# A two-layer PixArt block on one core: cross-attention's transfers in quarters, biases added one stage later, packed modulations

## The chip, the cores and the metric

The kernel runs on one core of one Trainium2 chip. The metric is the device time of one execution in microseconds. The core has five engines with an instruction queue each: TensorE (PE) for matrix products, VectorE (DVE), ScalarE (ACT), GpSimd (POOL) and SyncE (SP), which here only issues transfers (DMA). An engine works through its own queue in order and waits for semaphores where an instruction needs the work of another engine or of a transfer. POOL and ACT issue transfers too.

## The reference, cut to what matters

All numbers are float32. B = 8 batches, N = 512 rows, H = 512, 16 heads of 32, a context of 77 rows per batch, MLP width 2048.

```python
# layer 0 (stage x): adaptive layer norm, cross-attention to the context, residual
ss = silu(cond) @ W_ss + b_ss; scale, bias = split(ss, 2)     # for q and for kv
xq  = (1 + scale_q) * ln(x)  + bias_q
xkv = (1 + scale_kv) * ln(ctx) + bias_kv
x = x + (attention(xq @ Wq + bq, xkv @ Wkv + bkv) @ Wp + bp)
# layer 1
shift_a, scale_a, gate_a, shift_m, scale_m, gate_m = split(silu(cond) @ W_mod + b_mod, 6)
# stage a: self-attention
x = x + gate_a * (self_attention(ln(x) * (1 + scale_a) + shift_a) @ W_proj + b_proj)
# stage c: cross-attention
x = x + (attention(ln(x) @ W_qc + b_qc, ln(ctx) @ W_kvc + b_kvc) @ W_cproj + b_cproj)
# stage m: MLP
h = gelu((ln(x) * (1 + scale_m) + shift_m) @ W_mlp1 + b_mlp1)
x = x + gate_m * (h @ W_mlp2 + b_mlp2)
```

## The kernel before

**Stages.** Setup (0 to about 78 us of the span) computes the modulations of layer 0 and the keys and values of the context for layer 0. Then come stage x (to about 420), stage a (to about 1320), stage c (to about 1680) and stage m. Each stage runs over the 8 batches. The residual x lives in DRAM between stages, one buffer `xa` per batch (512x512). A stage loads a batch's x into an SBUF tile (`x_x`, `x_a`, `x_c`, `x_m`), and adds its result to `xa` with accumulating transfers that POOL issues (L734, L1094).

**Who sets the order.** Most engines' orders are written out by hand: the code's order is the engine's order (`manual_schedule`). In setup only PE's is, and in the context part too; in stages x and c all but SP's. What is not written out is set by the planner.

**Modulations.** `mod_half` (L95) and `Modulation.block` (L1400) compute silu(cond) @ W for 512 columns: four products with a stationary matrix of 128x8 (`csT`), one behind the other into the same 8 rows of PSUM, a copy on ACT, then four transposes and an addition of the bias on DVE. The two blocks of gates go to DRAM (`gate_a`, `gate_m`) instead. There are ten blocks: four in setup, four in stage x, two in stage c.

**Setup.** The context's rows (`cx`) come over ACT's queue, the weights over SP's. DVE takes the statistics of `cx` (L376), and copies `csT` out of PSUM (L169). `context_x` normalises, transposes and modulates the context, and multiplies it by the value weights (`cv_ps_x`, L359) and the key weights (`ckT_ps_x`, L408).

**Stages x and c** (`cross_phase`, L593). The loop is over 32 groups: batch b, group fc of four heads. A group computes scores, maxima, exponentials, sums (`total`, DVE), the division (POOL), a turn (DVE), and the outputs of the group before. Beside it run products with seven multiplications instead of eight (`Seven`), for the queries of the next batch or the projection of an older one, or a block of modulations (`fill`). The x of batch b+3 is loaded by one transfer at group 1, the value rows of the next batch (`load_values`) at group 2, stage x copies the input to `xa` at group 1, and `add_bias` (L743) adds the output bias to `xa` with one accumulating transfer of 1024 KB at group 3.

**Stage a** (`self_phase`, L1013). Again 32 groups. In a group, PE makes the scores of the next group for four tiles of 128 keys (`scores`, L1120), in two PSUM tiles that are free again when ACT has copied them (L1138) and DVE has taken the running maxima (`mx_a`, L1140). The maxima travel to DRAM (`mxd`), POOL issues eight accumulating transfers that subtract them from the scores in SBUF (`shift`, L1174), ACT takes exponentials (L1183), POOL and DVE add up (L1190). In group 2 the next batch's x is turned, and after that `load_x` (L1033) brings the x of the batch after it into the one tile `x_cur`; in group 3 DVE takes its statistics (L205), between the maxima of key tile 1 and those of key tile 2. The projection's result is biased on DVE (L1088), gated on POOL (L1091) and added to `xa` (L1094).

**Stage m.** `hidden` and `outputs` use products in quadrants with seven multiplications (`Quad`): a Quad takes up to four PSUM banks out of six in turn, and DVE empties them. `outputs` makes eight results of 128x256 (`result`, L1688): DVE reads PSUM into `res` (three buffers), adds the bias; POOL multiplies by the gate (L1696) and adds to the piece `xr` of the residual (L1697); SP stores `xr` (L1698), and after each of the first four results loads the piece for four results later (L1685) into one of the four `xr` buffers. The next batch's x is loaded at the start of `outputs` (L1538), normalised after the second set of products, turned on DVE and with 16 small transfers (L1551).

Of the kernel before, what the change touches and what calls it, by code (L numbers as in the profile page):

```python
# [11 lines left out]
F32 = mybir.dt.float32  # L12
# [12 lines left out]
SCALE = HD ** -0.5  # L25
RSQRT_SEED = float(0x5F3759DF)
# [3 lines left out]
def tile_pixart_block(ctx: ExitStack, tc: tile.TileContext, a: dict, out: bass.AP):  # L30
# [50 lines left out]
    csT = const.tile([P, KC, B], F32, name="csT")  # L81
# [13 lines left out]

    def mod_half(u, w, bname, dst, pool, psp, tag):
# [3 lines left out]
        for k in range(KC):  # L100
            nc.tensor.matmul(
                ps[:B, :], lhsT=csT[:, k, :], rhs=w[:, k, :], start=(k == 0), stop=(k == KC - 1)
            )
        m = pool.tile([B, H], F32, tag="mod", bufs=2, name=f"mod_{bname}_{u}")
        mark = nc.scalar.copy(m, ps[:B, :])
        yield
        pt = psp.tile([P, H], F32, tag=tag, name=f"modT_ps_{bname}_{u}")
        for j in range(KC):
            nc.tensor.transpose(pt[:, ts(j, B)], m[:, ts(j, P)], ident[:B, :B])
# [11 lines left out]
    def load_context(pool):  # L121
        cx = pool.tile([P, CT, H], F32, tag="cx", bufs=1, name="cx")
        rows = ctx_in.rearrange("b s h -> (b s) h")
        nc.scalar.dma_start(
            out=cx[:, : CT - 1, :],
            in_=rows[: (CT - 1) * P, :].rearrange("(t p) h -> p t h", p=P),
        )
        nc.scalar.dma_start(out=cx[:RL, CT - 1, :], in_=rows[(CT - 1) * P :, :])
        return cx
# [19 lines left out]

    kv_x = tc.alloc_tile_pool(name="kv_x", bufs=1)  # L150
    sp = tc.alloc_tile_pool(name="setup", bufs=1)
    with tc.tile_pool(name="setup_ps", bufs=2, space=PSUM) as spp:
# [11 lines left out]
        nc.scalar.activation(cs, c_sb, AF.Silu)  # L164

# [3 lines left out]
        nc.vector.tensor_copy(csT.rearrange("p k b -> p (k b)"), cp[:, : KC * B])  # L169

        w_ss_kv = [load_w("L0_xcond_Wss_kv", u) for u in range(2)]
        halves = [
            mod_half(u, w_ss_kv[u], "L0_xcond_bss_kv", mod_kv, sp, spp, "ps") for u in range(2)
        ]
        next(halves[0])
        bp = spp.tile([P, H], F32, tag="ps", name="bcol_ps")
        nc.tensor.transpose(bp[:, :n_cols], brow, ident[:n_cols, :n_cols])
        nc.vector.tensor_copy(bcol, bp[:, :n_cols])

# [7 lines left out]
        w_ss_q = [load_w("L0_xcond_Wss_q", 0)]  # L187
        w_l0 = [None, load_w("L0_xcond_Wkv", 1)]
        w_l0[0] = load_w("L0_xcond_Wkv", 0)
        w_ss_q.append(load_w("L0_xcond_Wss_q", 1))  # L190
# [158 lines left out]
    with tc.tile_pool(name="ps_s", bufs=2, space=PSUM, reuse_waits="tile") as ps_s:  # L349
# [17 lines left out]
        def context_x(eps, w_k, w_v, bkv, work, prep, cx):  # L367
# [4 lines left out]
            mv = small.tile([P, CT, 2], F32, tag="cmv", bufs=1, name="cmv_x")  # L372
            nc.gpsimd.memset(mv, 1.0)
            for t, n in enumerate(parts):
                bn = small.tile([P, 6], F32, tag="st", name=f"cst_x_{t}")
                nc.vector.bn_stats(bn[:n], cx[:n, t, :])  # L376
                nc.vector.bn_aggr(mv[:n, t, :], bn[:n])
# [3 lines left out]
            for k in range(KC):  # L381
# [14 lines left out]
                if k % 2:  # L396
                    mark = run(mod_half(k // 2, w_ss_q[k // 2], "L0_xcond_bss_q", mod_q, prep, ps_m, "m"))
            vd = dram.tile([R, H], F32, name="cvd_x")
            for t in range(CT):
# [3 lines left out]
                ))  # L403
            for j in range(KC):
# [12 lines left out]
            return kT, vd, last, mark, mv  # L417
# [168 lines left out]
        def cross_phase(  # L586
# [8 lines left out]
            bq, bkv, bo = names  # L595
            work = stack.enter_context(tc.tile_pool(name=f"work_{nm}", bufs=2, reuse_waits="tile"))
# [12 lines left out]
            def load_values(b):  # L609

                vr = st[b]["vr"] = work.tile([P, KB, H], F32, tag="vr", bufs=2, name=f"vr_{nm}{b}")
                whole = KB if b + 1 < B else KB - 1
                for i in range(QB):
                    at = vd[b * S : b * S + whole * SQ, :]
                    nc.sync.dma_start(
                        out=vr[ts(i, SQ), :whole, :], in_=at.rearrange("(k s) h -> s k h", s=SQ)
                    )
                    if whole < KB:
                        nc.sync.dma_start(
                            out=vr[i * SQ : i * SQ + S - whole * SQ, whole, :],  # L620
                            in_=vd[b * S + whole * SQ : (b + 1) * S, :],
                        )
# [89 lines left out]
            def project(b, j, room=None):  # L712
# [28 lines left out]
                )  # L741

            def add_bias(b):  # L743
                nc.gpsimd.dma_start(
                    out=x_dst[nm][b], in_=bo.partition_broadcast(N), accum_op=ALU.add
                )
# [120 lines left out]
            g.most(lambda: run(head[0]))  # L867
# [12 lines left out]
            ahead = behind_o = nothing  # L880
            for n in range(B * KC):
# [4 lines left out]
                if fc == 1 and more:  # L886
                    side = ahead
                elif b > 0 and fc == (2 if more else 1):
# [27 lines left out]
                now.scores()  # L916
                if pending:
                    pending.c22()
                    pending.mm(3)
                    pending.take("c12")  # L920
# [24 lines left out]
                now.total(0)  # L945
# [33 lines left out]
                if fc == 0 and more:  # L979
                    ahead = x_sums(b + 1, nc.gpsimd)  # L980
                    pump(ahead)
                if fc == 1 and b + 3 <= B:
                    load = next_x(nc.sync)
                if fc == 2 and more:
                    load_values(b + 1)
                if fc == 1 and modulated:
                    with tc.issue_after(load.ins):
                        nc.sync.dma_start(out=x_dst[nm][b], in_=x_src[nm][b])
                if fc == 3:
                    add_bias(b)  # L990
# [22 lines left out]
        def self_phase(w, bo_row, work, work_2, ctx_c):  # L1013
# [8 lines left out]
            x_cur = x_sb["a", 0]  # L1022
            sums = [xpool.tile([P, 4, N], F32, tag="x", name=f"sum_a{i}") for i in range(2)]
# [9 lines left out]
            def load_x(b):  # L1033
                nc.scalar.dma_start(
                    out=x_cur, in_=x_src["a"][b].rearrange("(t p) d -> p t d", p=P)
                )

# [43 lines left out]
            def project(b, t):  # L1081
                if t == 0 and b + 1 < B:
# [704 lines left out]
```

## Time and profile before

| | us |
|---|---|
| median of 3 runs (2483.24 to 2492.29) | 2483.47 |
| the profiled execution | 2482.09 |
| its span, first to last instruction | 2480.3 |
| PE busy, in all | 2355.1 |
| PE busy, setup, 0 to 78 | 57.4 |
| PE busy, stage x, 78 to 420 (342 us) | 326.3 |
| PE busy, a stretch of stage a, 560 to 1160 (600 us) | 581.3 |
| PE busy, stage c, 1320 to 1680 (360 us) | 333.1 |
| PE busy, stage m, 1800 to 2400 (600 us) | 600.0 |

The span is that of one profiled execution. A busy time is the sum of an engine's instructions; the clock column of the windows is the share of TensorE's full clock that the chip granted (1.00 is full). Timelines give the start and length of merged instructions, the tile written and the tiles read, and in brackets how long the engine had been idle and who released it. Transfers of the queue q0 (software, issued by POOL) move 176 MB, those of q1 (SP) 108 MB.

### The profile page before, as it was taken

The numbers are of one execution on the slowest core, as the hardware profiler recorded it, in microseconds if no ns is written. First come the engines' busy times: TensorE is split into PE (matmuls) and PEld (weight loads), VectorE is DVE, ScalarE is ACT, GpSimd is POOL, SyncE is SP. The second block draws the span as 40 slices with busy tenths as digits, with TensorE's granted clock in tenths as the row PEclk, the third lists the DMA queues.
The fourth block names the chain that finished last, engine by engine and source line by source line (L and its number), as shares of the span: only waits on it lengthen the run. The fifth ranks groups of instructions, "written<-read, shape, count | busy, mean of one in ns | idle before, by whom it ended". The sixth has DMA issues, their size and how long they took to land. (4 is left out here: it accounts for less than half of the span.)

```text
span 2480.3 us, 44498 instructions
## 1 busy us (share of the span) xinstructions
PE 2355.1 (95%) x17701; PEld 1502.9 (61%) x17701; DVE 1690.7 (68%) x2922; ACT 1168.3 (47%) x2043; POOL 1179.3 (48%) x1210
## 2 busy tenths in 40 slices
PE   7899999889999999999988899998999999999998
PEld 3567776323333333333234677777888888888887
DVE  3577785588888888888745777766656556655563
ACT  1366663577777777776652565652121121121120
POOL 2357674366776777867664566654202102012011
PEclk9999999999999999999999899999999999999999
DMA  7456647498999999999996465554211111112010
GB/s 262 145 118 145 146 67 123 98 183 169 194 190 182 199 172 193 190 180 181 199 218 168 88 112 83 78 85 115 58 32 56 45 45 56 34 47 66 23 51 26
DMA packets 142595, 298.99 MB, mean 121 GB/s; under 512 B 15668, under 2 KB 46468, under 8 KB 142260
## 3 DMA queue, kind: packets, MB, share of 16 engines
q0 software_dynamic: 59424, 176.23, 41.5%
q1 hardware_dynamic: 77023, 108.16, 14.6%
q10 hardware_dynamic: 5941, 11.76, 1.4%
q8 instruction: 139, 2.28, 0.4%
q14 instruction: 68, 0.56, 0.1%
HBM read 252.39 MB, written 61.54 MB: 127 GB/s over the span
## 5 line engine op out<-in xcount | busy, mean ns | idle before, releaser
L1696 POOL TENSOR_TENSOR res_m<-res_m,gate_m 128x256 f32<-128x256 f32 x64 | 49.9, 780 | 638.8 <-DVE res_m L1694 638.8
L1174 POOL DMA_DIRECT2D e_a<-mxd_a x256 | 249.7, 2043 | 155.1 <-DMA mxd_a<-mxT_a 142.8
L1183 ACT ACTIVATE e_a<-e_a 128x1024 f32<-128x1024 f32 x256 | 265.8, 1058 | 87.1 <-DMA e_a<-mxd_a 86.2
L1138 ACT COPY e_a<-sT_a 128x1024 f32<-128x1024 f32 x256 | 254.9, 1010 | 94.0 <-DVE mx_a L1140 45.6
L1630 ACT ACTIVATE hT<-hT,bcol 128x512 f32<-128x512 f32 x128 | 91.9, 721 | 239.1 <-DVE hT L1605 231.0
L1190 POOL TENSOR_TENSOR sum_a<-e_a,e_a 128x1024 f32<-128x1024 f32 x64 | 153.7, 2445 | 103.5 <-ACT e_a L1183 103.1
L1190 POOL TENSOR_TENSOR sum_a<-sum_a,e_a 128x1024 f32<-128x1024 f32 x64 | 171.7, 2693 | 3.8 <-ACT e_a L1183 3.8
L1140 DVE TENSOR_TENSOR mx_a<-sT_a,mx_a 128x1024 f32<-128x1024 f32 x128 | 151.0, 1218 | 31.7 <-PE sT_a L1120 28.7
L1120 PE MATMUL sT_a<-qT_a,kT_a 32*128 32x512 f32 x1024 | 150.1, 640 | 12.3 <-ACT e_a L1138 10.6
L1200 PE MATMUL o_ps_a<-e_a,v 128*32 128x512 f32 x1024 | 148.5, 611 | 9.2 <-ACT e_a L1183 9.0
L807 POOL TENSOR_TENSOR p_x<-p_x,sm_x 128x616 f32<-128x616 f32 x64 | 83.6, 1421 | 103.3 <-DVE sm_x L803 81.7
L1597 PE MATMUL q_ps_h<-x_m,w_L_xcond_W_mlp 128*128 128x256 f32 x512 | 132.3, 381 | 0.0
L1597 PE MATMUL q_ps_h<-xT_m,w_L_xcond_W_mlp 128*128 128x256 f32 x512 | 131.7, 380 | 0.0
L304 PE MATMUL q_ps_a<-xnT_a,w_L_xcond_W_qkv 128*128 128x512 f32 x256 | 124.1, 613 | 6.9 <-ACT xnT_a L1043 6.9
L807 POOL TENSOR_TENSOR p_c<-p_c,sm_c 128x616 f32<-128x616 f32 x64 | 83.0, 1403 | 99.0 <-ACT xnT_c L293 40.9
L1218 DVE RECIPROCAL rz_a<-z_ps_a 128x512 f32<-128x512 f32 x32 | 107.4, 3358 | 31.3 <-PE z_ps_a L1211 31.3
L1597 PE MATMUL q_ps_h<-x_m,w_s 128*128 128x256 f32 x512 | 122.0, 381 | 5.3 <-DVE w_s L1522 4.5
L304 PE MATMUL k_ps_a<-xnT_a,w_L_xcond_W_qkv 128*128 128x512 f32 x256 | 120.5, 608 | 0.0
L312 PE MATMUL v_ps<-w_L_xcond_W_qkv,xnT_a 128*128 128x512 f32 x256 | 120.0, 612 | 0.0
L312 PE MATMUL proj_ps_a<-w_L_xcond_W_proj,oT_a 128*128 128x512 f32 x256 | 117.9, 604 | 1.4 <-DVE oT_a L1221 1.4
L1597 PE MATMUL q_ps_y<-w_L_xcond_W_mlp,h_s 128*128 128x256 f32 x512 | 113.1, 379 | 0.0
L1597 PE MATMUL q_ps_y<-w_L_xcond_W_mlp,hT 128*128 128x256 f32 x512 | 113.1, 379 | 0.0
(421 smaller groups left out, 5271.8 us busy)
## 6 DMA issues: line engine op xcount, KB each, us to landing
e_a<-mxd_a POOLq DMA_DIRECT2D x256, 512.0 KB, 11.6
xa<-in_L_xcond_bp_dram POOLq DMA_DIRECT2D x8, 1024.0 KB, 14.6
xa<-res_x POOLq DMA_DIRECT2D x32, 256.0 KB, 5.1
xa<-res_a POOLq DMA_DIRECT2D x32, 256.0 KB, 14.3
x_c<-xa SPq DMA_DIRECT2D x8, 1024.0 KB
w_L_xcond_W_mlp<-in_L_xcond_W_mlp_dram SPq DMA_DIRECT2D x8, 1024.0 KB
xa<-in_L_xcond_b_cproj_dram POOLq DMA_DIRECT2D x8, 1024.0 KB, 15.2
xa<-res_c POOLq DMA_DIRECT2D x32, 256.0 KB, 5.2
```

The source lines that it names most:

```text
L304: nc.tensor.matmul(ps, lhsT=w[:, k, ts(j, P)], rhs=xT[k], start=(k == 0), stop=(k == KC - 1))
L312: nc.tensor.matmul(ps, lhsT=xT[k][:, cols], rhs=w[:, k, :], start=(k == 0), stop=(k == KC - 1))
L807: nc.gpsimd.tensor_tensor(v, v, self.sm[i].unsqueeze(3).to_broadcast([P, 2, NT, S]), ALU.mult)
L1120: nc.tensor.matmul(sc[h // 2][:, h % 2, :], lhsT=kT[ts(h, HD), ts(k, P)], rhs=qT[ts(h, HD), :], start=True, stop=True,)
L1138: nc.scalar.copy(self.e[k][i], sc[i])
L1140: nc.vector.tensor_tensor(self.mx[1 - i], sc[1 - i], self.e[0][1 - i] if k == 1 else self.mx[1 - i], ALU.max,)
L1174: nc.gpsimd.dma_start(out=self.e[k][i].rearrange("p h n -> p (h n)"), in_=self.mxd[2 * i : 2 * i + 2, :] .rearrange("h n -> (h n)").partit ...
L1183: nc.scalar.activation(self.e[k][i], self.e[k][i], AF.Exp)
L1190: engine.tensor_tensor(sum_i, self.e[0][i] if k == 1 else sum_i, self.e[k][i], ALU.add)
L1200: nc.tensor.matmul(self.po[ts(h, HD), :], lhsT=vt[:, self.fc * P + h * HD : self.fc * P + (h + 1) * HD], rhs=self.e[k][h // 2][:, h % 2, : ...
L1218: nc.vector.reciprocal(r, self.pz)
L1597: nc.tensor.matmul(self.banks[n][:, half], lhsT=lhsT, rhs=rhs, start=(k == 0), stop=(k == len(pairs) - 1),)
```

## The change

- **Transfers of stages x and c.** The load of x, of the value rows and the copy to `xa` are cut in four, one part for each group of a batch, each held by a dependency (`paced`) until a certain sum of that group is done on DVE. SP's order in these stages is now written out too.
- **Biases.** `add_bias` of `cross_phase` is gone: `xa` no longer has the output bias of stages x and c. Stage a adds `bp` to its x on POOL, and to its result through a row `gate * b_proj + bp` per batch (`shift`). Stage m adds `b_cproj` with accumulating transfers: four into each `x_cur`, one into each piece `xr`. The first x of the next stage, loaded ahead in group loop 5, gets its bias by one transfer a group (`owed`).
- **Modulations.** `csT` is padded to 32 columns; the four products of a block write four groups of 32 rows of PSUM, each on its own. A matrix of ones and zeros (`pick`, 128x8) adds the four groups up in the products that also turn the columns (`mod_columns`). The second block of stage c moves from group (1, 0) to (1, 1).
- **Setup.** PE's and DVE's order is written out: `csT` is copied before the context's statistics; the context comes first on SP's queue; both modulations of kv start before the bias columns; the modulations of q stand between the value products.
- In the first batch of stages x and c the sums of the next batch's xT go to DVE instead of POOL.

```diff
+    def mod_parts(ps, w):
         for k in range(KC):
             nc.tensor.matmul(
-                ps[:B, :], lhsT=csT[:, k, :], rhs=w[:, k, :], start=(k == 0), stop=(k == KC - 1)
+                ps[ts(k, CG), :], lhsT=csT[:, k, :], rhs=w[:, k, :], start=True, stop=True
             )
+    def mod_columns(ps, m):
+        for j in range(KC):
+            nc.tensor.matmul(ps[:, ts(j, B)], lhsT=m[:, ts(j, P)], rhs=pick, start=True, stop=True)
...
-        nc.scalar.dma_start(
+        nc.sync.dma_start(
             out=cx[:, : CT - 1, :],
...
+    def paced(after, dma):
+        if after is not None:
+            tc.add_manual_dep(
+                dma.ins, after.ins.name,
...
+    def add_row(dst, row):
+        nc.gpsimd.dma_start(out=dst, in_=row.partition_broadcast(P), accum_op=ALU.add)
...
+        nc.vector.memset(csT, 0.0)
+        nc.vector.tensor_reduce(
+            pick, ident.rearrange("p (g c) -> p c g", c=CG)[:, :B, :], AX.X, ALU.add
+        )
...
+        context_rows(cx, c_mv)
         next(halves[0])
+        next(halves[1])
...
             for t in range(CT):
                 run(values_c(
...
+                for half in queries_mod[t - 1 : t]:
+                    next(half)
+                for half in queries_mod[t - 2 : t - 1] if t > 1 else []:
+                    run(half)
...
-                    ahead = x_sums(b + 1, nc.gpsimd)
-                    pump(ahead)
-                if fc == 1 and b + 3 <= B:
-                    load = next_x(nc.sync)
-                if fc == 2 and more:
-                    load_values(b + 1)
-                if fc == 1 and modulated:
-                    with tc.issue_after(load.ins):
-                        nc.sync.dma_start(out=x_dst[nm][b], in_=x_src[nm][b])
-                if fc == 3:
-                    add_bias(b)
+                    ahead = x_sums(b + 1, nc.gpsimd if b else nc.vector)
+                    pump(ahead, 1 if b else 0)
+                if b + 3 <= B:
+                    if fc == 0:
+                        ahead_x[b] = next_x_tile()
+                    dst, src = ahead_x[b]
+                    paced(half, nc.sync.dma_start(out=dst[:, fc, :], in_=src[ts(fc, P), :]))
+                    if b + 3 == B:
+                        owed = dst[:, fc, :], bo
+                if fc and more:
+                    load_values(b + 1, [fc - 1], last)
+                elif b and fc == 0:
+                    load_values(b, [QB - 1], last)
+                if modulated:
+                    for t in [fc] if more else [[0, 1], [2, 3], [], []][fc]:
+                        paced(last, nc.sync.dma_start(out=x_dst[nm][b][ts(t, P), :], in_=x_src[nm][b][ts(t, P), :]))
...
+            def add_bias(t):
+                nc.gpsimd.tensor_tensor(x_cur[:, t, :], x_cur[:, t, :], bp_row, ALU.add)
+
+            def gate_and_shift(b):
+                g = st[b]["g"] = gate_rows(gate_a, b, work, "a")
+                shift = st[b]["shift"] = work.tile([P, H], F32, tag="shift", name=f"shift_a{b}")
+                nc.gpsimd.tensor_tensor(shift, g, bo_row, ALU.mult)
+                nc.gpsimd.tensor_tensor(shift, shift, bp_row, ALU.add)
...
-                        nc.vector.tensor_tensor(tmp, pr, bo_row, ALU.add)
+                        nc.vector.tensor_tensor(tmp, pr, st[b]["g"], ALU.mult)
                         def add():
-                            nc.gpsimd.tensor_tensor(tmp, tmp, st[b]["g"], ALU.mult)
+                            nc.gpsimd.tensor_tensor(tmp, tmp, st[b]["shift"], ALU.add)
...
                 for k in range(1, NT):
                     g.shift(k)
                 flush(0)
                 flush(1)
+                if fc == 3 and b + 2 < B:
+                    for t in range(NT):
+                        add_bias(t)
+                if fc == 0 and b:
+                    gate_and_shift(b - 1)
...
-                    (0, 1): lambda: mod.block(4), (1, 0): lambda: mod.block(5),
+                    (0, 1): lambda: mod.block(4), (1, 1): lambda: mod.block(5),
...
                     in_=x_src["m"][b][ts(i, P), :].rearrange("(t c) d -> c t d", c=SQ),
                 )
+            for t in range(NT):
+                add_row(x_cur[:, t, :], bc)
...
                 nc.sync.dma_start(out=xr, in_=x_src["m"][b][ts(t + 2 * r, P), ts(c, H2)])
+                add_row(xr, bc[ts(c, H2)])
                 pieces[t, r, c] = xr
```

## The prediction

> **What bounds the kernel now.** I read the page's totals first, then the windows by stage, then the timelines of single engines inside one round of each stage.
>
> ```profile
> PE 2355.1 (95%) x17701; PEld 1502.9 (61%) x17701; DVE 1690.7 (68%) x2922; ACT 1168.3 (47%) x2043; POOL 1179.3 (48%) x1210
> 0.00:78.00 78.00, 57.40 (x193) 28.46 (x194) 21.64 (x68) 13.61 (x22) 19.18 (x31) 1.00 0.65 225
> 160.00:420.00 260.00, 255.35 (x4228) 199.59 (x4228) 197.12 (x370) 155.35 (x430) 169.40 (x219) 1.00 0.62 113
> 660.00:760.00 100.00, 97.31 (x428) 32.09 (x430) 84.81 (x99) 73.19 (x82) 75.64 (x56) 1.00 0.97 186
> 1800.00:2000.00 200.00, 200.00 (x929) 176.05 (x928) 117.11 (x278) 38.19 (x63) 24.86 (x32) 1.00 0.18 49
> ```
>
> TensorE (PE) is idle for only 125 us of 2480.3: 20.6 of them in the first 78 us, 15.7 in cross-attention x, 27 in cross-attention c (1320 to 1680), about 3 per batch in self-attention, none in the MLP until its tail. So little can be won, and whatever makes PE wait in self-attention or the MLP is paid in full.
>
> Self-attention, third batch, fourth group (VectorE DVE, then GpSimd POOL, then PE):
>
> ```profile
> 750.48 0.68 DVE L205 BATCH_NORM_STATS2 st_a<-x_a 128x6 f32<-128x512 f32 x1
> 753.58 0.18 DVE L206 BATCH_NORM_AGGREGATE mv_a<-st_a 128x2 f32<-128x6 f32 x1
> 753.84 2.36 DVE L1140 TENSOR_TENSOR mx_a<-sT_a,mx_a 128x1024 f32<-128x1024 f32 x2
> ...
> 752.43 6.02 POOL L1174 DMA_DIRECT2D e_a<-mxd_a  x6
> 762.31 4.82 POOL L1190 TENSOR_TENSOR sum_a<-e_a,e_a 128x1024 f32<-128x1024 f32 x2 [3.86 <-ACT e_a L1183]
> ...
> 756.58 1.14 PE L1120 MATMUL sT_a<-qT_a,kT_a 32*128 32x512 f32 x8
> ```
>
> The statistics of the next-but-one batch's x stand on DVE ahead of the maxima of key tile 2; the scores of tile 3 on PE (756.58) need the PSUM those maxima free (done 756.20). Slack: 0.4 us.
>
> **The change, part by part. (1) Self-attention: the bias on x.** After the change POOL adds bp to x_cur (four 128x512 adds), after all eight shift transfers of the fourth group, and the four statistics on DVE wait for them; batches 0 to 5 have this step. The shifts are out at 752.43+6.02 = 758.45. An add of that shape on POOL takes 1.26 (rows sq_x, to_x): four end at 763.5. The last statistic and its aggregate take 0.84, so DVE comes to the maxima at 764.4 instead of 753.84: 10.5 late. Behind it wait two maxima, two sums, two maxima and the transposes that PE's next mxT needs; none has slack (DVE is busy without a gap from 753.84 to 766.5). PE: 10.5-0.4 = 10.1, plus 0.3 for the semaphore hops. The statistics began 7 to 8 us before the shifts' end in all six batches (545.2/552.0, 647.8/655.2, 853.5/860.9, 956.2/964.0, 1059.2/1066.8), so 6 x 10.4 = 62. After a wait PE is also slow for a while:
>
> ```profile
> 119.30 2.04 PE L507 MATMUL sa_ps_qx<-xs_x,sq_x 128*128 128x256 f32 x4 [3.48 <-ACT p_qx L705]
> 121.14 1.91 PE L507 MATMUL sb_ps_qx<-xs_x,sq_x 128*128 128x256 f32 x4
> ```
>
> The same four take 1.03 to 1.13 otherwise. Summing such excesses: 2.6 us after this gap, 1.6 after one at 1374, 4.5 after one at 1405, 1.8 after the first 10.6 us. I take 2.0: 6 x 12.4 = 74; bounds 57 (9.5 each, no slow clock) and 96 (11.5+4.5).
>
> The Trainium skill, "TensorE: Matmul & The Clock Gate", Part 1, says that an idle window of about 3.4 us halves the clock until a busy window of the same length has passed: by it each such stall would cost 1.7 more and the part 72. The trace already shows slow matmuls (1.86 for 1.03) after a gap of 2.16 at 1643.9, so the row is harsher.
>
> The gate's edits: DVE multiplies where it added, POOL adds where it multiplied (same shapes, nothing). gate*bo+bp is two POOL operations, 2.5 us a batch, in the idle 5.36 before the sums of the first group (788.25): nothing; without that cover 8 x 2.5 = 20.
>
> **(2) MLP: the bias of cross-attention, on POOL's queue.** After each load of an xr piece POOL issues an accumulating transfer. For pieces 4 to 7 it stands between result n and result n+1: POOL waits for xr's load, which waits for the store of result n out of the same buffer, which waits for POOL's own add.
>
> ```profile
> 1782.38 0.55 SPq L1698 DMA_DIRECT2D out_dram<-xr  x1
> 1784.32 0.34 SPq L1685 DMA_DIRECT2D xr<-xa  x1
> ...
> 1795.63 0.42 DVE L1605 TENSOR_TENSOR res_m<-q_ps_y,u_y 128x256 f32<-128x256 f32 x1 [1.48 <-PE q_ps_y L1597]
> ...
> 1802.27 1.89 PE L1597 MATMUL q_ps_h<-x_m,w_s 128*128 128x256 f32 x8
> ...
> 2450.83 0.34 SPq L1698 DMA_DIRECT2D out_dram<-xr  x1
> 2452.55 0.32 SPq L1685 DMA_DIRECT2D xr<-xa  x1
> ```
>
> Store to next load: 1.72 to 1.94. The load's landing: about 2.2 (issued 1784.32; the 1 us windows show data to 1787.1). Issue on POOL: 0.9 (row xa<-res_a at 707.56). Two POOL steps: 1.6. One round: 6.5. SP is busy with the 16 xT transfers until 1782.38, then four rounds: the sum for result 4 ends at 1808.4. Result 7 reuses result 4's res buffer (three buffers), so DVE reads its PSUM bank at 1808.4 instead of 1795.63, 12.8 late; results 5 and 6 are 3 and 9 late. Six banks in turn: result 7's bank is the one that the next batch's second Quad needs at 1803.13 (product 5, inside the row of 1802.27), 7.1 after 1796.05. PE stalls 5.7, with 1.6 of slow clock (the 1374 case) 7.3; seven batches: 51. In the last batch SP is free: 2450.83+4 x 6.5 = 2476.8, then three results of 1.6: 2481.6 for 2475.0: 6.5. Together 57. Bounds: 10 (a round of 5.3 leaves 1 a batch, 3 at the tail) and 90 (bank taken one Quad earlier, 11 a batch, tail 10).
>
> The skill's "DMA: Bandwidth & Descriptors", Anatomy of one DMA, gives about 2 us plus bytes/436e3 for a transfer and says that the issuing sequencer does the waiting; 131072 bytes would be 2.3 for each leg, the round 7.1, and the sum 19 more. It is the rule that speaks most against this edit.
>
> The four adds into x_cur at the batch's change: loads are over at 1848.5 (1 us windows), four issues of 1.0, landing 5.1 (row xa<-res_x): 1857.6, before the statistics at 1858.52. Nothing; by the loaded row (14.3) DVE would be 8 late.
>
> **(3) Packed modulations and setup.**
>
> ```profile
> 15.59 5.37 PE L101 MATMUL od_ps_L_xcond_bss_kv<-w_L_xcond_Wss_kv,csT 128*8 128x512 f32 x8 [10.59 <-DVE csT L169]
> 38.67 17.43 PE L359 MATMUL cv_ps_x<-w_L_xcond_Wkv,cT_x 128*128 128x512 f32 x40
> ...
> 753.67 1.06 PE L1200 MATMUL o_ps_a<-e_a,v 128*32 128x512 f32 x8
> ```
>
> PE's first product waits for csT, which DVE copies only after context statistics that wait for cx (12.98). A block's four products take 3.60 in a row; four in four column groups of the array take 1.06 (o_ps_a). The columns' step lies between 0.41 (the transposes of before) and 1.5 (eight weight loads of 0.19); I take 1.5, since the weights are now 128x128. So 1.4 a block, ten blocks, where PE is the limit.
> Setup: the queue puts cx first; 1.26 MB at the 322 GB/s of the first 20 us is 4 us, then 3.3 for each weight: second modulation's products at about 13 (not 21.97), its columns by 18, then rsqrt 2.6, normalise 2.4, transposes and evacuations some 3.5: values from about 26.5. From there 17.43+16.75 (keys)+5.55 (x transposes)+2 x 2.6 (query modulations between) = 71.4 instead of 78.08: gain 7, bounds 0 and 12.
> Cross-attention x: four blocks, two of them in groups where PE waits for DVE anyway, about -5; against it the sums of xT for batch 1 move to DVE, 4 x 0.68, in the group whose chain ends in the 3.48 gap above: net -3, bounds +5 and -9. Cross-attention c: the second block leaves (1, 0), where PE waits 3.33 at 1405.66 and then runs slow (4.5); it costs 2.6 in (1, 1): -5, bounds 0 and -9.
> **At nothing:** the quartered loads of x, value rows and copies, held until a group's sums. SP now stands at these waits, and behind it are later quarters, weight loads and the gate's store; each is used a group (12 us) or more later. Without that cover a late quarter would cost a wait of some 3 us per group. The 16 bias transfers into DRAM go (1.07 us of POOL each, POOL at 65%), 8 short ones replace them.
>
> Sum: +74+57-7-3-5 = +116 on the profiled execution, 2482.09 us (span 2480.3 and 1.8 around it; 1.4 under the median of the runs, 2483.47): **2598 us**.
>
> **Rivals.** *MLP round hidden:* if the banks come round later than I count or the round is near 5.3, only the self-attention stall stays: 2482+74-15+10 = 2551. For it: DVE is at 58% there; against: DVE stands in order, and result 7 is 12.8 late with 7.1 of slack. *Self-attention stall hidden, MLP paid:* 2482+57-15 = 2524; it needs POOL's adds done before 750.5, but its shifts end at 758.45. *The packed blocks don't overlap:* four products at 0.9 and dearer columns give back 15 us: 2613. *Faster:* the setup alone decides. If cx and the first weights land as early as one queue allows (values at 21 to 22, 12 us, with the upper gains of x and c, 18) and both stalls together cost under 15 us, the time is 2465 or so. It turns on one place: POOL's four adds in the fourth group; only if POOL reaches them by about 751, 12 us earlier than the row, does PE not wait. Nothing in the trace does that.
>
> **How the numbers follow.** Forecast (both stalls) 0.70, of which the unpacked blocks 0.05; MLP hidden 0.16; self hidden 0.08; faster 0.04; within 0.5% (12 us, about what a measurement of this kernel tells from no change) 0.02. Low end 2530: self 62 (no slow clock), MLP 15, gains 29 of at most 30, which takes in the rival of 2551; high end 2645: self 90, MLP 80, gains 7. Both leave out about 2 in 10. Slower by over 0.5%: 0.70+0.16+0.08 = 0.94.
>
> **What would show it.** On DVE a wait of about 8 to 10 us before the x_a statistics, released by POOL's adds, six times, with PE idle as long before the fourth scores; PE at 87 to 90% in the self-attention windows. On POOL, in the MLP, waits for xr's load between results, DVE's last res_m 12 us later, PE's share under 100% in 1800 to 2400. The value products in setup at 26 rather than 38.7. I am wrong if PE stays at 97% and 100% there.

## The result: 155 us slower

The changed kernel took 2639.24 us (median of 4 runs, 2639.01 to 2642.69), the kernel before, beside it, 2484.28: a ratio of 1.062 with a 95% interval of 1.0596 to 1.0643. The profiled execution has a span of 2637.5 us, 157.2 more than before. The time lies inside the stated range, 41 us above the prediction of 2598.

First the same totals and windows as were shown of before (windows: start to end, length, busy time and count of PE, its weight loads, DVE, ACT and POOL, granted clock, share of the DMA engines, GB/s):

```profile
PE 2388.0 (91%) x17737; PEld 1528.0 (58%) x17737; DVE 1712.1 (65%) x2933; ACT 1166.1 (44%) x2045; POOL 1292.8 (49%) x1329
0.00:78.00 78.00, 63.61 (x249) 38.39 (x249) 28.44 (x83) 16.84 (x28) 21.32 (x31) 0.98 0.66 224
160.00:420.00 260.00, 254.66 (x4116) 198.77 (x4115) 195.49 (x368) 155.33 (x430) 164.05 (x215) 1.00 0.45 100
660.00:760.00 100.00, 86.38 (x367) 28.79 (x367) 81.61 (x93) 65.09 (x74) 69.18 (x53) 0.95 0.82 159
1800.00:2000.00 200.00, 184.72 (x814) 159.24 (x815) 107.82 (x255) 30.91 (x53) 47.77 (x59) 0.94 0.33 64
```

From 660 to 760 (stage a) PE was busy for 97.3 of 100 us, from 1800 to 2000 (MLP) for 200 of 200; now it is 86.4 and 184.7, at a granted clock of 0.95 and 0.94. Its busy time grew too (2355 to 2388; 10 of it in stage a, 29 in the MLP, while stage c has 5 less): after a wait the matmuls take longer, as the rows below show.

To place the loss I read when certain products of PE start, and take the differences: *setup* is up to stage x's first scores, *x* and *c* run from the start of their first scores to that of their last outputs, *a* from its first scores to its last, *passage* from there to stage c's first scores, *MLP* from its first product to its last, *tail* from there to the end. The short stretches between (from x to a 30.6 us, from c to the MLP 19.3, both within 0.6 of before) are left out.

| us | setup | x | a | passage | c | MLP | tail | span |
|---|---|---|---|---|---|---|---|---|
| before | 91.3 | 317.2 | 809.4 | 98.9 | 324.7 | 781.4 | 8.3 | 2480.3 |
| after | 79.9 | 321.5 | 884.2 | 110.7 | 316.8 | 859.7 | 14.8 | 2637.5 |
| difference | -11.4 | +4.3 | +74.8 | +11.8 | -7.9 | +78.3 | +6.5 | +157.2 |

**Stage a.** The fourth group of the third batch again, from the timelines of DVE, POOL and PE (start, length, what, and in brackets the idle time before it with its releaser):

```profile
779.61 0.69 DVE L252 BATCH_NORM_STATS2 st_a<-x_a 128x6 f32<-128x512 f32 x1 [8.36 <-POOL x_a L1096]
780.82 0.69 DVE L252 BATCH_NORM_STATS2 st_a<-x_a 128x6 f32<-128x512 f32 x1 [0.30 <-POOL x_a L1096]
...
784.08 2.32 DVE L1204 TENSOR_TENSOR mx_a<-sT_a,mx_a 128x1024 f32<-128x1024 f32 x2
...
772.20 6.09 POOL L1238 DMA_DIRECT2D e_a<-mxd_a  x6
775.56 7.66 POOL L1096 TENSOR_TENSOR x_a<-x_a,bp_row 128x512 f32<-128x512 f32 x4
...
786.42 2.11 PE L1184 MATMUL sT_a<-qT_a,kT_a 32*128 32x512 f32 x8 [9.09 <-ACT e_a L1202]
788.46 3.43 PE L351 MATMUL q_ps_a<-xnT_a,w_L_xcond_W_qkv 128*128 128x512 f32 x4
```

The shifts end at 778.3 and the four additions stand behind them (their row begins earlier, but DVE can start on the first result at 779.6, then on one every 1.2 us). DVE stands 8.36 us before the first statistic and 0.30 before each other one, the maxima come late, and PE's scores of tile 3 wait 9.09. They then take 2.11 (1.14 without a wait), the four products behind them 3.43 (1.98). The six gaps are 10.29, 9.81, 9.09, 9.58, 9.21 and 9.59, together 57.6.

**MLP.** The end of its first batch, timelines of DVE, POOL, SP and PE:

```profile
1877.17 0.42 DVE L1676 TENSOR_TENSOR res_m<-q_ps_y,u_y 128x256 f32<-128x256 f32 x1 [6.00 <-POOL xr L1769]
1884.26 0.42 DVE L1676 TENSOR_TENSOR res_m<-q_ps_y,u_y 128x256 f32<-128x256 f32 x1 [6.20 <-POOL xr L1769]
...
1874.69 0.89 POOL L179 DMA_DIRECT2D xr<-in_L_xcond_b_cproj_dram  x1 [4.44 <-DMA xr<-xa]
1875.31 1.02 POOL L1768 TENSOR_TENSOR res_m<-res_m,gate_m 128x256 f32<-128x256 f32 x1
1876.42 0.72 POOL L1769 TENSOR_TENSOR xr<-xr,res_m 128x256 f32<-128x256 f32 x1
...
1877.17 0.34 SPq L1770 DMA_DIRECT2D out_dram<-xr  x1
1878.98 0.32 SPq L1756 DMA_DIRECT2D xr<-xa  x1
...
1877.65 2.08 PE L1668 MATMUL q_ps_h<-xT_m,w_L_xcond_W_mlp 128*128 128x256 f32 x4 [4.02 <-DVE res_m L1676]
1879.52 1.91 PE L1668 MATMUL q_ps_h<-x_m,w_s 128*128 128x256 f32 x4
1884.74 2.08 PE L1668 MATMUL q_ps_h<-x_m,w_s 128*128 128x256 f32 x4 [3.31 <-DVE res_m L1676]
```

POOL stands 4.44 us before the bias of one piece, waiting for that piece's load. Its two steps for the result come behind it; then SP stores the piece and loads the next one into the same buffer, and so round after round. From store to store SP's rows give 7.35, 7.36, 6.89 and 7.08 us. Results 6 and 7 are read late out of two PSUM banks, and PE waits twice. Four matmuls last 1.9 to 2.1 us instead of 1.03, and between the two gaps PE does not return to its speed.

**The passage to stage c.** POOL's and PE's timelines, first of the kernel before, then of the changed kernel:

```profile
1282.97 2.40 POOL L1190 TENSOR_TENSOR sum_a<-e_a,e_a 128x1024 f32<-128x1024 f32 x1 [3.01 <-ACT e_a L1183]
...
1304.43 1.06 PE L1211 MATMUL z_ps_a<-sum_a,ones 128*32 128x512 f32 x8
```

```profile
1367.94 1.26 POOL L1101 TENSOR_TENSOR shift_a<-gate_a,row_L_xcond_b_proj 128x512 f32<-128x512 f32 x1 [18.72 <-DMA gate_a<-gate_a]
1369.29 1.26 POOL L1102 TENSOR_TENSOR shift_a<-shift_a,bp_row 128x512 f32<-128x512 f32 x1
1370.51 4.66 POOL L1254 TENSOR_TENSOR sum_a<-e_a,e_a 128x1024 f32<-128x1024 f32 x2
...
1380.99 2.97 PE L1275 MATMUL z_ps_a<-sum_a,ones 128*32 128x512 f32 x8 [7.32 <-DVE sum_a L1254]
```

The last batch's row `gate * b_proj + bp` stands on POOL ahead of the last group's sums and waits 18.72 us for its gate. Before, POOL had no such step there: its sums began as soon as ACT's exponentials were ready, and PE's product of the sums had no wait.

### The profile page after: what moved, and what is told of

Read it like the earlier page. It is cut to its first block, busy times and chain, and to the rows that moved or that the text cites. A ratio compares the mean times of both kernels' runs of the same rounds, so it can differ in the third digit from the quotient of the medians.

```text
span 2637.5 us, 44912 instructions
## 1 busy us (share of the span) xinstructions
PE 2388.0 (91%) x17737; PEld 1528.0 (58%) x17737; DVE 1712.1 (65%) x2933; ACT 1166.1 (44%) x2045; POOL 1292.8 (49%) x1329
## 5 line engine op out<-in xcount | busy, mean ns | idle before, releaser
L1701 ACT ACTIVATE hT<-hT,bcol 128x512 f32<-128x512 f32 x128 | 91.3, 722 | 324.7 <-DVE hT L1676 318.2
L1184 PE MATMUL sT_a<-qT_a,kT_a 32*128 32x512 f32 x1024 | 156.2, 671 | 78.1 <-ACT e_a L1202 76.4
L179 POOL DMA_DIRECT2D xr<-in_L_xcond_b_cproj_dram x64 | 57.2, 1140 | 229.9 <-DMA xr<-xa 218.9
L1668 PE MATMUL q_ps_h<-x_m,w_s 128*128 128x256 f32 x512 | 136.0, 410 | 31.0 <-DVE res_m L1676 24.8
L1668 PE MATMUL q_ps_h<-xT_m,w_L_xcond_W_mlp 128*128 128x256 f32 x512 | 141.1, 400 | 23.0 <-DVE res_m L1676 23.0
L179 POOL DMA_DIRECT2D x_m<-in_L_xcond_b_cproj_dram x32 | 29.8, 1327 | 241.0 <-DMA x_m<-xa 240.8
L1184 PEld LDWEIGHTS sT_a<-qT_a,kT_a 32*128 32x128 f32 x1024 | 42.9, 190 | 177.7 <-ACT e_a L1202 101.2
L1768 POOL TENSOR_TENSOR res_m<-res_m,gate_m 128x256 f32<-128x256 f32 x64 | 56.2, 877 | 178.7 <-DVE res_m L1766 178.7
L351 PE MATMUL q_ps_a<-xnT_a,w_L_xcond_W_qkv 128*128 128x512 f32 x256 | 132.4, 648 | 6.3 <-ACT xnT_a L1109 6.3
L1668 PEld LDWEIGHTS q_ps_h<-x_m,w_s 128*128 128x128 f32 x512 | 103.5, 205 | 53.4 <-DVE res_m L1676 29.8
L1668 PEld LDWEIGHTS q_ps_h<-xT_m,w_L_xcond_W_mlp 128*128 128x128 f32 x512 | 102.0, 201 | 40.7 <-DVE res_m L1676 25.8
## 6 DMA issues: line engine op xcount, KB each, us to landing
e_a<-mxd_a POOLq DMA_DIRECT2D x256, 512.0 KB, 11.7
```

The source lines that it names most:

```text
L351: nc.tensor.matmul(ps, lhsT=w[:, k, ts(j, P)], rhs=xT[k], start=(k == 0), stop=(k == KC - 1))
L1184: nc.tensor.matmul(sc[h // 2][:, h % 2, :], lhsT=kT[ts(h, HD), ts(k, P)], rhs=qT[ts(h, HD), :], start=True, stop=True,)
L1668: nc.tensor.matmul(self.banks[n][:, half], lhsT=lhsT, rhs=rhs, start=(k == 0), stop=(k == len(pairs) - 1),)
L1701: nc.scalar.activation(dst, src, AF.Gelu_apprx_tanh, bias=bias_cols("L1_xcond_b_mlp1", 1, j))
```

## The experiments

All are built from the changed kernel unless it says otherwise. A `-` line is the changed kernel's. Chips differ: in the four sets of runs the kernel before took 2486.63, 2488.41, 2498.67 and 2488.22 us, so a ratio is to the runs beside it, and stages are compared by the table at the end of this section. Where several of these kernels have the same code in a stage, its length still differs by some microseconds: x is 321.5 to 325.4 in six of them, a 884.2 to 888.1 in three, the MLP 853.1 to 859.7 in four. Smaller differences than these tell nothing.

### e1, e2, e3: the biases back in DRAM

The lines that the three share, without the condition on the stage:

```diff
+            def add_bias(b):
+                nc.gpsimd.dma_start(
+                    out=x_dst[nm][b], in_=bo.partition_broadcast(N), accum_op=ALU.add)
...
+                if fc == 0 and b:
+                    add_bias(b - 1)
+                if fc == 3 and not more:
+                    add_bias(b)
```

e1 does this in stage x alone and takes `add_bias(t)` and `gate_and_shift` out of stage a (the result is biased and gated as before); e2 in stage c alone, without `add_row` in the MLP; e3 does both.

> The changed kernel, with the bias of stage x added to the residual in DRAM as before (one accumulating transfer of 1024 KB per batch), so that stage a has neither the four adds on POOL nor the row gate*b_proj+bp. My theory (POOL's adds behind the shifts hold DVE's statistics, and the row of the last batch holds POOL before the last sums): stage a wins back its 75 us and the passage to stage c about 10, so 2639-85 = 2554 (2545 to 2565), and the six gaps of 9 to 10 us on PE in front of the fourth scores are gone. Rival (stage a is late because the transfers of the shifts are slower beside other traffic, the place of the adds being chance): under 40 us won, gaps stay.

> The changed kernel, with the bias of stage c added in DRAM as before, so that the MLP has no accumulating transfers. My theory (POOL waits in its queue for the load of each xr piece): the MLP wins back all of its 78 us and the tail its 6.5, so 2639-85 = 2554 (2548 to 2562), PE at 100% in the MLP's windows. Rival (only the 48 us of waiting go, and the slow matmuls in the MLP have a cause of their own): 2591.

> Both biases in DRAM as before; transfers in four parts, packed modulations and the setup stay as changed. If the two bias edits are the whole loss: 2639-170 = 2469, that is about 15 us under the kernel before (ratio 0.994, 2462 to 2476). Rival (pacing or packing cost something that the stalls hide): 2484 or more.

Measured: e1 2561.32, e2 2566.65 (one run each), e3 2491.43, ratio to before 1.0034 (1.0000 to 1.0068). Stage a is back at 809.0 in e1, the passage at 100.6, the MLP at 781.1 in e2. So the 75 us of stage a and the 78 of the MLP come from just these edits. The times are worse than that: e2 lies 5 above its range, since its stage c is 9.0 longer than in the changed kernel, and e3 was expected at 2469 and came out where the rival had it. Its stages x and c are 331.9 and 324.8, 10 and 8 longer than in the changed kernel, though the rival's reasons, pacing and packing, are in both kernels. Timelines of e3's POOL and PE show where:

```profile
377.32 1.03 POOL L793 DMA_DIRECT2D xa<-in_L_xcond_bp_dram  x1
...
387.44 0.48 PE L553 MATMUL sa_ps_ox<-w_L_xcond_Wp,os_x 128*128 128x256 f32 x1
389.89 1.65 PE L553 MATMUL sa_ps_ox<-w_L_xcond_Wp,os_x 128*128 128x256 f32 x3 [1.96 <-issue]
391.33 1.91 PE L553 MATMUL sb_ps_ox<-to_x,oT_x 128*128 128x256 f32 x4
```

Inside one product's four matmuls PE stops for 1.96 us without a releaser in the timeline ("issue"); the stop ends 12.6 us after POOL has issued a bias transfer of 1024 KB, and then PE runs slowly. The next longest gap of this kind in e3's stage x (1.27 us, up to 357.80) ends 13.8 us after such an issue, the longest in e2's stage c (3.89, up to 1587.04) 15.2 us; the changed kernel's stages x and c have none over 0.4 us. Against the changed kernel e3's stage x has 3.5 us more of gaps and 6.8 more of busy time. The last section comes back to these stops.

### e4: one addition for four

```diff
                 if fc == 3 and b + 2 < B:
-                    for t in range(NT):
+                    for t in range(1):
                         add_bias(t)
```

> The changed kernel with only the first of POOL's four adds in each of the six batches; the layer norm of the other three quarters of x in batches 2 to 7 then lacks bp. If the place behind the shifts sets the wait: the first statistic waits as long as before, only the three waits of 0.3 behind it go, about 1.1 us a batch: 2632 (2628 to 2637). If the adds' own time sets it: three quarters of the wait go, 45 us: 2595.

Measured: 2626.90, one below the range. Stage a is 875.8, that is 8.4 less, 1.4 a batch; the MLP, whose code is the changed kernel's, happens to be 6.6 shorter. Waits of DVE in stage a (us in total, times, longest), first the changed kernel, then e4:

```profile
DVE st_a L252 <- POOL x_a L1096: 58.5, 24, 9.5
```

```profile
DVE st_a L252 <- POOL x_a L1096: 51.6, 6, 9.0
```

Three quarters of the work are gone and seven eighths of the wait stay. It is the place in POOL's queue, not the additions' own time.

### e5, e6: the bias as an addition on POOL in stages x and c

```diff
                 def done(r):
                     t = j + 2 * r
+                    nc.gpsimd.tensor_tensor(res[t], res[t], b_row, add)
                     nc.gpsimd.dma_start(
```

Stage a and the MLP then add nothing. e6 also puts `Modulation.block` back to four products in a row and four transposes.

> The changed kernel with both biases put on the result of the cross-attentions by one POOL addition (128x512, 1.26 us) in front of the store that POOL issues, 32 in stage x and 32 in stage c; no bias transfer of 1024 KB, and nothing added in stage a or the MLP. If the bias edits are the loss and the 1024 KB transfers are what made e3's stages x and c 11 and 8 us longer than the changed kernel's: 2486.5-19 = 2468 for the profiled span, ratio to before about 0.994 (2462 to 2478). Rival (the additions hold up POOL's divisions and so DVE's turns and PE): stages x and c as long as in e3 or longer, 2485 or more.

> e5 with the six blocks of modulations of stages x and c as before (four products one behind the other, 3.60 us, and four transposes), the four of setup packed. If the blocks only fill PE's wait for DVE's turn (gaps of 4.95 and 2.35 us in front of the outputs, with slow matmuls behind them): the gaps shrink by about 2.5 each and stages x and c get some 4 us shorter each, e5 minus 8. Rival (PE is the limit there, as my prediction had it): e5 plus 6 to 15.

Measured: e5 2511.14, ratio 1.0078 (1.0049 to 1.0106); the rival was right. Stages x and c are 336.1 and 334.9 long: PE's waits for DVE's turns (`pw`), which come behind POOL's divisions, grew from 7.3 us in two places to 14.0 in 17 and 18.4 in 18. From 160 to 420 POOL is busy for 75% of the time in e5, for 63% in the changed kernel. e6 took 2506.72 in one run, 4.4 under e5, which neither expectation has: stage x 3.1 shorter, stage c 3.2 longer. Packed or not makes no difference that this can tell.

### e7: the MLP's additions deferred

```diff
-                add_row(xr, bc[ts(c, H2)])
+                if n < 4:
+                    add_row(xr, bc[ts(c, H2)])
+                elif n == 7:
+                    for i in range(4, 7):
+                        ti, ri, ci = order[i]
+                        add_row(pieces[ti, ri, ci], bc[ts(ci, H2)])
+                    add_row(xr, bc[ts(c, H2)])
```

> The changed kernel with the same 64 accumulating transfers in the MLP, but those of pieces 4 to 7 issued together behind POOL's work on result 3, when their loads have long been under way, and not each between two results. If it is the chain of a round (store, load, landing, issue, two POOL steps; 7.2 us, four times in a row) that makes the MLP late: 60 to 78 us are won, 2639-70 = 2569 (2558 to 2582). Rival (the transfers themselves, or the slow matmuls, cost the time): under 20 won, 2620.

Measured: 2555.89. The MLP takes 780.7, and PE is busy all the time (windows of e7, columns as above):

```profile
1880.00:2080.00 200.00, 200.00 (x929) 176.26 (x928) 116.78 (x283) 37.80 (x63) 47.91 (x60) 1.00 0.35 71
```

With the same 64 transfers, all 78 us and the tail (7.5) are back, somewhat more than expected. The chain of rounds is the whole cost.

### e8, e9: stage a's steps in other places

In e8 the four additions stand ahead of `g.shift(0)`, where POOL has just finished a sum. In e9 they stay, the statistics move behind the maxima of the whole group, the last batch's row moves behind the last sums, and the MLP is e7's:

```diff
-                if fc == 3 or (b, fc) == (0, 0):
+                if (b, fc) == (0, 0):
                     next(ln, None)
                     next(ln, None)
...
                 nxt.maxima()
+                if fc == 3:
+                    next(ln, None)
+                    next(ln, None)
...
-            gate_and_shift(g.b)
             fills = [ctx_c.values(3), ctx_c.values(4), ctx_c.keys(0)]
...
+            gate_and_shift(g.b)
             w_c = [load_w("L1_xcond_W_qc", 0, queue=nc.scalar)]
```

> The changed kernel with POOL's four adds of a fourth group in front of its eight shifts and not behind them. If the place in POOL's queue sets DVE's wait: the statistics no longer wait 8 to 9 us; the adds take 5 us where POOL is idle for about 3.2, so the shifts go out some 2 us later; of the 75 us of stage a 45 to 65 come back: 2639-55 = 2584 (2574 to 2596). Rival (POOL is full and any place costs the same): 2630 or more.

> The changed kernel, nothing computed elsewhere, three steps moved: the four statistics of a fourth group stand on DVE behind the maxima (behind key tile 3) and not ahead of key tile 2; the row gate*b_proj+bp of the last batch is made behind the last sums and not in front of them; the MLP's adds as in e7. If the three waits are the whole loss of these stages: stage a 820 for 884 us (1 to 2 us a batch remain, since the next transpose of the maxima comes later), the passage to stage c 11 shorter, the MLP 781: span 2637-64-11-83 = 2479 (2472 to 2494), about the time before. Rival (the later statistics hold up the maxima's transpose in full, 3.4 us a batch or more with slow matmuls): stage a 845 or more, span above 2505.

Measured: e8 2604.14, 8 above its range; stage a is 846.1, so that 38 of the 75 came back (for the rest see the last section). e9 2527.10, ratio 1.0103 (1.0079 to 1.0128): the passage is 99.0 and the MLP 781.2, as the theory has it, but stage a is 870.0. Here the rival won, and the waits of PE in stage a of e9 say how:

```profile
PE o_ps_a L1264 <- ACT e_a L1247: 22.2, 8, 3.5
PE sT_a L1184 <- ACT e_a L1202: 19.4, 11, 3.3
...
PE v_ps L359 <- DVE mxT_a L1228: 11.1, 6, 2.1
```

The waits of 9 to 10 are gone; in their place are waits for the exponentials (`o_ps_a`, 5.0 in the changed kernel's stage a) and for the maxima's reduction (`mxT_a`), which now stands behind the statistics.

### e10, e11: blocks, sums and pacing on top of e9

e10 takes e9 with `x_sums` of the first batch on `nc.gpsimd` again and the blocks of e6; e11 is e9 with `paced` adding no dependency.

> e9 with the sums of the first batch on POOL again and the six blocks of stages x and c unpacked as before. If DVE's sums and the missing 2.5 us of products make the gaps of 4.95 and 2.35 in front of the outputs: the gaps fall under 1, stages x and c get 4 to 7 us shorter each, e9 minus 8 to 14. Rival (the wait only changes its place, as e6's mixed signs hint): within 4 of e9.

> e9 without the dependencies that hold the quarters until a group's sums; SP's written order stays. My prediction put pacing at nothing: stages x and c within 3 us of e9. Rival (unheld transfers fall on PE's instruction supply or on other loads): 8 us or more longer together.

Measured: e10 2523.60, ratio 1.0100 (1.0068 to 1.0131), its span 3.3 us under e9's, as the rival had it. The two `pw` gaps, 7.3 us in stage x of e9, are gone, yet stage x is only 4.0 shorter and stage c 1.9: PE now waits 4.0 us in three places for ACT's copy of a block (`mod`). The wait has for a good part changed its place. e11 took 2531.53 in one run, stage x 4.2 and stage c 1.1 longer than e9. That is between the two expectations and about as much as the same code differs by, so pacing is worth some 5 us at most, and no effect of it is shown.

### e12: the bias back in DRAM, in quarters

```diff
+            def add_bias(b, t):
+                nc.gpsimd.dma_start(out=x_dst[nm][b][ts(t, P), :],
+                    in_=bo.partition_broadcast(P), accum_op=ALU.add)
...
+                if nm == "x" and b:
+                    add_bias(b - 1, fc)
+                if nm == "x" and not more and fc > 1:
+                    add_bias(b, 2 * fc - 4)
+                    add_bias(b, 2 * fc - 3)
```

With stage a of e1, the MLP of e7, and blocks and sums of e10.

> The changed kernel with bp back in DRAM, but by four transfers of 256 KB a batch, one a group, behind POOL's divisions (so stage a has neither the adds nor the row); the MLP's adds deferred as in e7; sums on POOL and blocks unpacked as in e10. From e1's parts (stage a 809, passage to stage c 100.6), e7's MLP (781, tail 7.5) and e10's gain of 6 in stages x and c: 2559.5-74-9-6 = 2471 with e1's stage x of 333; with a stage x of 318 to 322, if it was the size of the 1024 KB transfers that made it longer, 2457 to 2461. Range 2452 to 2476, ratio to before 0.988 to 0.998. Rival (POOL's issues of 0.9 us, four a batch for one, hold up the divisions as e5's additions did): stage x 333 or more, 2475 or more, no gain on before.

Measured: 2466.49 (2465.52 to 2468.83), ratio to before 0.9913 (0.9888 to 0.9938). It beats both kernels; against the table of the result, what it has less than the kernel before is setup (9.4 us) and stage c (9.6), and no other stage is more than 1.1 us longer. Stage x is 318.3, 14.5 shorter than in e1, of which e10's step may explain 4; PE has no stop of over 0.4 us without a releaser in it. So in e12 the stops went with the transfers of 1024 KB. Whether it is their size or their place in the group (they moved as well) was not tried apart, and the kernel before, which issues the same eight transfers in its stage x at another place, has a stage x of 317.2 and one such stop, of 0.46 us.

| us | setup | x | a | passage | c | MLP | tail |
|---|---|---|---|---|---|---|---|
| e1 | 77.8 | 332.8 | 809.0 | 100.6 | 317.5 | 855.1 | 16.7 |
| e2 | 80.2 | 324.3 | 888.1 | 109.0 | 325.8 | 781.1 | 6.4 |
| e3 | 80.8 | 331.9 | 811.5 | 98.3 | 324.8 | 780.8 | 8.4 |
| e4 | 80.7 | 325.4 | 875.8 | 108.9 | 316.7 | 853.1 | 14.5 |
| e5 | 80.4 | 336.1 | 814.6 | 97.7 | 334.9 | 782.9 | 6.8 |
| e6 | 79.5 | 333.0 | 810.4 | 94.8 | 338.1 | 785.4 | 6.8 |
| e7 | 79.7 | 323.2 | 885.0 | 111.2 | 316.8 | 780.7 | 7.5 |
| e8 | 79.7 | 323.7 | 846.1 | 112.1 | 316.7 | 859.6 | 14.5 |
| e9 | 77.4 | 322.3 | 870.0 | 99.0 | 315.6 | 781.2 | 6.8 |
| e10 | 79.7 | 318.3 | 867.1 | 101.6 | 313.7 | 782.1 | 6.9 |
| e11 | 79.3 | 326.5 | 868.5 | 100.6 | 316.7 | 780.7 | 7.5 |
| e12 | 81.9 | 318.3 | 810.3 | 98.5 | 315.1 | 781.6 | 9.0 |

The stretch from x to a, which the table leaves out, is 5 to 6 us longer in e5 and e6 than in the others.

## Why the prediction was right in kind and 41 us short

- **Both stalls: right.** e1 and e7 each take one of them away, and the stage returns to its length of before.
- **Stage a, +74 predicted, +74.8 measured.** That it is so near is partly chance: the gap was 9.6 on average, not 10.4; slow matmuls and the rest cost 2.9 a batch, not 2.0. The two rows behind the gap at 786.42 show 2.4 us of slow matmuls (2.11 for 1.14, 3.43 for 1.98). The estimate of 1.7 us, worked out from the idle window that the Trainium skill states ("TensorE: Matmul & The Clock Gate", Part 1), is under that.
- **The MLP's body, +51 predicted, +78.3 measured: the mechanism right, the term mis-sized most.** The step that failed is "One round: 6.5." It is 7.2: from store to next load 1.8 to 2.3, not 1.72 to 1.94, and from the load's issue to POOL's next issue 2.5 to 2.8, not 2.2. Over four rounds this delays result 7 by 2.7 more. Result 6's bank is late enough to count as well; the prediction's own 9 us for it were already over the 8.0 that its bank had to spare (read until 1793.40, needed at 1801.40 in the kernel before). So there are two gaps a batch (47.8 us in 14) for one of 5.7, and some 4.4 us of slow matmuls and the like for 1.6: the second gap comes before the matmuls are back at their speed. The estimate from the Trainium skill's page "DMA: Bandwidth & Descriptors" (Anatomy of one DMA), a round of 7.1 and 19 us more, was nearer than the rows I took. The page's fit is for transfers that GpSimd issues, though, and the store and the load here are SP's.
- **The tail, +6.5 predicted, +6.5 measured, partly by chance:** POOL's rounds are 7.0 to 7.3 here too, and its last addition ends 11.5 us after the start of PE's last matmul, 8.5 later than before; what follows it is 2 us shorter.
- **The passage, +11.8: not in the sum.** The step that failed: "gate*bo+bp is two POOL operations, 2.5 us a batch, in the idle 5.36 before the sums of the first group (788.25): nothing". The last batch has no such group behind it; its row stands ahead of the last sums and waits for a load. e9 moves that step and gets the 11.7 back.
- **Setup, -7 predicted, -9.0 to the first query products.** Values started at 24.4, predicted 26.5.
- **Stage x, -3 predicted, +4.3 from its first scores** (setup and x together, to the last output: -10 predicted, -7.1 measured). The step that failed: "1.4 a block, ten blocks, where PE is the limit". The packed products do take 1.06 for 3.60, but PE was not the limit there. The group's timelines of PE in the kernel before, then of PE and DVE in the changed kernel:

```profile
106.25 3.60 PE L1410 MATMUL mod_ps<-w_L_xcond_W_mod,csT 128*8 128x512 f32 x8
...
110.40 1.48 PE L828 MATMUL s_x<-pw_x,vr_x 32*32 32x128 f32 x92 [0.21 <-ACT p_x L796]
```

```profile
94.77 1.06 PE L102 MATMUL mod_ps<-w_L_xcond_W_mod,csT 128*32 128x512 f32 x8
100.79 2.90 PE L872 MATMUL s_x<-pw_x,vr_x 32*32 32x128 f32 x96 [4.95 <-DVE pw_x L860]
103.62 1.88 PE L109 MATMUL modT_ps<-pick,mod 128*128 128x8 f32 x8
...
97.17 0.68 DVE L688 TENSOR_TENSOR xs_x<-xnT_x 128x512 f32<-128x512 f32 x1
...
99.77 1.83 DVE L860 STREAM_TRANSPOSE pw_x<-p_x 128x768 f32<-128x768 f32 x2
```

  The four sums that moved to DVE (97.17 to 99.77) stand ahead of its turn; PE used to fill that time with the block's 3.60, and now waits 4.95 and then takes 2.90 for outputs that took 1.48. With sums and blocks as before the gap is gone (e10); which of the two makes how much of it was not tried apart.
- **Stage c, -5 predicted, -7.9 measured, for another reason, so the near number is luck.** The step that failed: "the second block leaves (1, 0), where PE waits 3.33 at 1405.66". PE's waits for DVE's turn did not go but grew, to 7.3 us in two places, and unpacked blocks make stage c 3.2 longer in e6 and, with the sums moved, 1.9 shorter in e10: no gain is shown. What the change wins there is the removal of the 1024 KB bias transfers, which the prediction put under "at nothing": with them stage c is 325.8 and 324.8 (e2, e3), without them 316.8.
- **Pacing at nothing:** not refuted; e11, one run, leaves up to 5 us open.
- Of the x_cur additions, "nothing" was right: no statistic of the MLP waits.

## What to carry to other kernels

Work that is put "one stage later" has to be placed, not only counted: the same additions cost 78 us of the MLP between two steps of a chain and nothing behind it (e7); in stage a one addition behind the shifts makes DVE wait nearly as long as four (e4), and four ahead of the shifts cost half (e8). Before a product is made shorter, look at what PE would wait for next: a slow product ahead of a wait can be free. Of the places tried for the bias of stage x, the cheapest was DRAM, in quarters behind POOL's divisions (e12), and for that of stage c the MLP with the additions behind the chain (e7).

## What was not expected of the hardware

PE stops in the middle of its work without a releaser in the timeline. In stages x and c of all the kernels there are 21 such stops of over 0.4 us, up to 3.89. Of these, 17 lie in stages that have bias transfers of 1024 KB (the kernel before, e1, e2, e3), but four do not: one of 1.16 us in e4 and three of 0.75 to 0.98 in e11. The kernels with these transfers also scatter more: 2480.0 to 2500.3 us for the kernel before and 2465.5 to 2468.8 for e12 beside it, 2484.0 to 2510.0 for e3. The quarters of e12 had no such stop.

The traces' records of transfers say more than the timelines. There is a queue of kind "instruction" (q8) with packets of 16 KB, 39 of them in each of these stages, one in some 8 us. Each of the 21 stops ends 1.24 to 1.59 us after such a packet has ended. In the 1.6 us around the packet of the stop shown for e3, POOL's transfers (q0) take 69% of the time of the 16 DMA engines:

```profile
q0 software_dynamic: 74, 0.15, 68.9%
q8 instruction: 1, 0.02, 5.2%
```

So PE most likely waits there for its next instructions. What makes these come late, and whether the bias transfers do, was not tried.

DVE's smallest operations lasted up to 2.8 us in e8's stage a, usually 0.16. These three stand beside POOL's issues of the shifts and its row for the next gate (DVE's timeline in the first group of a batch):

```profile
681.09 1.17 DVE L275 TENSOR_TENSOR lnt_a<-lnt_a,lnv_a 128x4 f32<-128x4 f32 x1
682.30 0.17 DVE L277 SCALAR_TENSOR_TENSOR lny_a<-lnt_a,lny_a 128x4 f32<-128x4 f32 x1
682.50 1.93 DVE L274 TENSOR_TENSOR lnt_a<-lny_a 128x4 f32<-128x4 f32 x1
```

In the kernel before, whose POOL has no row to make there, the first operation of this chain lasts 2.50 beside the shifts' issues, and these three take 0.16 each; in e8 PE then waits 3.82 before its next scores in this group. There are six such waits, one a batch, 3.6 to 4.0 us long and 22.9 together, and PE's busy time in e8's stage a is 16.6 above that of the kernel before. These are about the 37 us that e8 did not win back. That POOL's row is what slows DVE there was not tried by itself; the changed kernel has the same row, and its waits at these scores are 1.6 to 3.0.
